# Two graph-attention layers on one core: neighbour sums begun during the projection, for 17 targets in place of 13

## The chip, the core and the metric

The kernel runs as one program on one core of a Trainium2 chip. The core has a matrix engine (PE; PEld is its loading of weights), a vector engine (DVE), a scalar engine (ACT), GpSimd (POOL), a sync engine (SP) that here only issues transfers, and sixteen DMA engines shared by all queues. The metric is the device time of one execution in microseconds, as the median of the runs shown.

## What is computed

Two graph attention layers over N = 3327 nodes with 1024 features, each followed by a residual sum and a normalization. Layer 0 has 8 heads of 128, layer 1 has one head. The graph is sparse: a node has some 16 neighbours. Cut to what matters:

```python
h = (x @ W).reshape(C, H, D)                       # layer 0
e = leaky_relu(alpha_src[:, :, None] + alpha_dst[:, None, :], 0.2)
attn = softmax(where(adj == 0, -inf, e))           # per head
x = layernorm(x + concat_heads(attn @ h))
h = x @ W1                                         # layer 1
attn = softmax(where(adj > 0, leaky_relu(f1 + f2.T, 0.2), -9e15))
x = layernorm(x + relu(attn @ h))
```

## The kernel before

Nodes are handled in NT = 26 tiles of 128. The program has two arms and picks one by a flag that it computes (L923, L929); with these inputs the sparse arm runs. Its work falls into three stages.

**Projection (L514 to L926).** For each tile t, x is loaded three tiles ahead (`load_x`), transposed on PE (`flip`), and multiplied with W in three cuts (`project`, L546); `keep` takes the cuts out of PSUM with ACT (L560 to L565) and SP writes the tile's rows to the table `h0_d` in HBM (L568). The last 16 columns of a row hold the exponentials of the scores. Each cut calls `pace()` after every second multiply, so a tile has 12 slots. `pace` advances two generators that fill the time beside the multiplies:

- `listing` (L582) makes lists of edges, one target tile per round. The mask tile `ad` (3327 int32 columns of `adj`, turned to bytes by the POOL queue's transfer, `load_mask`, L535; three buffers) loses its own diagonal on POOL (`clear`, L339), is counted on ACT (`words`, L350, L352) and folded three times on DVE (L357) into words of 104. `ends` and `ends2` turn counts into places with one small PE multiply each (L366, L391), an ACT copy (L371, L392) and a row of small POOL operations. `keys` and `columns` take the largest of the keys on DVE (L309, L311); `ways`, `places`, `spread`, `give`, `take` and `sources` bring each edge to its slot (L451 on ACT, L470 on PE) and end with the row numbers `idx` (L511, DVE). In a round, mask t + 4 is cleared and counted. `factors` (L330 to L334, ACT and POOL) puts the target's scores beside the edges; `keep` calls it.
- `sums_so_far` (L629) starts when tile 13 is projected. The first 13 tiles of the table are then written, and edges are ordered so that blocks 0 and 1 of a target's four blocks (and one further block for what is left over) have their sources there. For the first EARLY = 13 targets it gathers these two blocks from `h0_d`, four indirect transfers each by POOL (L641), into a ring of three buffers, `near[1]`, `far`, `near[0]`; DVE makes the weighted marks `e` (L658 to L662), PE multiplies (L671, 32 multiplies a block, in the trace two records each; L719 and L737 for the denominators), and the half sum goes to `half_d` (L727). It fetches two blocks ahead and has 12 steps per target, one per slot.

What is left of both generators runs off behind the last projection (L924).

**Layer 0 (L1057 to L1200).** Targets run through a pipeline in an order written at L1381 to L1385. A late target (13 to 25) gathers blocks 0 to 3 with four indirect transfers each and the end block with one (L1034), 17 in all; an early one gathers blocks 2, 3 and the end, 9 in all, and reads its half sum (L1076). Each also reads x, its own row of h and a list, and writes `y_d`. Five buffers `src` hold gathered blocks. The order is late, early, late, early, for eleven pairs, then early 11 and 12, then late 24 and 25. L1168 on DVE is the start of a target's end.

**Layer 1 (L1202 to L1301)** gathers from `y_d` in the same way, sums (L1258) and multiplies with W1 (L1290). It waits for all of layer 0.

The engines work their instructions in program order. The order of the projection stage is what the calls of `pace` make of it at build time.

Of the kernel before, what the change touches and what calls it, by code (L numbers as in the profile page):

```python
# [9 lines left out]
F32 = mybir.dt.float32  # L10
# [9 lines left out]
P = 128  # L20
# [6 lines left out]
def kernel(  # L27
# [57 lines left out]
    EARLY = NTH  # L85
# [35 lines left out]
    cnt = const.tile([P, NT, 4], F32, name="cnt")  # L121
# [193 lines left out]
    class Edges:  # L315
# [6 lines left out]
        def __init__(self, ph, t):  # L322
            self.ph, self.t = ph, t
            self.d, self.deg, self.end2 = cnt[:, t, :2], cnt[:, t, 2:3], cnt[:, t, 3:]
# [18 lines left out]
        def words(self, ad, junk):  # L343
# [7 lines left out]
            self.deg_b = sbuf("deg_b", [P, 2], 4, dt=BF16)  # L351
            nc.scalar.activation(self.deg_b, self.d, AF.Copy)  # L352
            w = ad.bitcast(I32)
            for n in range(3):
                m = WD >> n
                half = sbuf(f"wd{n}", [P, m], 4 if n == 2 else 1, dt=I32)
# [6 lines left out]
        def ends(self, tri_b):  # L363
# [4 lines left out]
            end, off, low, high = (v[:, n : n + 2] for n in (0, 2, 4, 6))  # L368
            self.mid, self.over, self.offs = v[:, 8:10], v[:, 10:12], v[:, 12:14]
            self.more, self.mid2, self.start, self.off2 = (v[:, n : n + 1] for n in range(14, 18))  # L370
# [5 lines left out]
            nc.gpsimd.tensor_scalar(high, end, float(HG2), None, op0=OP.max)  # L376
            nc.gpsimd.tensor_tensor(self.over, high, low, OP.subtract)
            nc.gpsimd.tensor_tensor(self.more, self.over[:, :1], self.over[:, 1:], OP.add)
            nc.gpsimd.tensor_copy(self.more_b, self.more)
            nc.gpsimd.tensor_tensor(self.deg, self.d[:, :1], self.d[:, 1:], OP.add)  # L380
            nc.gpsimd.tensor_copy(self.offs, off)
            nc.gpsimd.tensor_tensor(self.offs[:, :1], off[:, :1], self.d[:, 1:], OP.subtract)
            nc.gpsimd.tensor_tensor(self.offs[:, :1], self.offs[:, :1], self.over[:, :1], OP.subtract)
            mv = self.ph.mvs[self.t % 4][:, :, : XB + 1 : XB]
            nc.gpsimd.tensor_copy(mv[:, 0, :], self.offs)
            nc.gpsimd.tensor_tensor(mv[:, 1, :], self.offs, mv[:, 0, :], OP.subtract)

        def ends2(self, all_b):
# [6 lines left out]
            nc.gpsimd.tensor_tensor(self.off2, self.start, self.d[:, 1:], OP.subtract)  # L395
            nc.gpsimd.tensor_tensor(self.off2, self.off2, self.over[:, 1:], OP.add)
# [117 lines left out]
    with ExitStack() as own, tc.manual_schedule():  # L514
        ph = Phase(own, "proj", {"A": 2, "T": 1})
        pool, bank = ph.pool, ph.bank
        part = Phase(own, "part", {})
        opening = ExitStack()
# [35 lines left out]
        def keep(t, c):  # L554
            if t not in hts:
                hts[t] = ph.sbuf("ht", [P, HW0], 3)
            ht, acc, c0 = hts[t], accs.pop((t, c)), CUTS0[c]
            m = min(CUTS0[c + 1], D) - c0
            if c == 2:
                nc.scalar.activation(sd0[:, t].rearrange("p a h -> p (a h)"), acc[:, m:], AF.Copy)  # L560
                lists[t].factors()
# [13 lines left out]
        def count(t):  # L575
            if t < NT:
                clear(t)
                lists[t].words(ads.pop(t), junk)
                if t:
                    load_mask(t + 2)  # L580
# [962 lines left out]
```

## Time and profile before

| what | value |
|---|---|
| median of 6 runs | 1913.58 us (1908.11 to 1918.13) |
| profiled execution | 1917.7 us, span 1916.0 us |
| granted TensorE clock, mean | 0.916 |
| busy share of the span | PE 86%, PEld 49%, DVE 62%, ACT 27%, POOL 57% |
| moved by DMA | 586.89 MB, 306 GB/s |
| share of 16 DMA engines | POOL queue (q0) 68.7%, SP queue (q1) 18.1% |

A page is one profiled execution; times are microseconds from the start of its span. A share of busy time is a mean over the stages. "Idle before" in a row of a group is time in which that engine did nothing just before an instruction of the group, with what ended most of it. In a table of waits, `PE dd L366 <- ACT deg_b L352: 11.6, 8, 3.1` reads: before its instruction at line 366, PE waited for what ACT makes at line 352, for 11.6 us in all, 8 times, at most 3.1 us. In the timeline a row has its start, how long it took, engine, line, operation, output and input.

### The profile page before, as it was taken

To read this page: it belongs to the slowest core of one execution; us is meant where nothing else is said; L and a number is where in the kernel's file an instruction comes from. 1 tells how busy PE (TensorE), PEld (TensorE's weight loads), DVE (VectorE), ACT (ScalarE), POOL (GpSimd) and SP (SyncE) were. 2 spreads that over 40 slices of the span, in tenths; PEclk is the share of its full clock that TensorE was granted. 3 is DMA by queue.
4 is the path that set the end of the run, shared out by engine and by line. 5 is a ranking of instruction groups with operands and counts; after the bars stand their busy time and mean duration, and the time that the engine had idled before them with its cause. 6 is when DMAs were issued, how large, how long until landed. Compare 5 with 4: busy or idle time off the path is not lost.

```text
span 1916.0 us, 35590 instructions
## 1 busy us (share of the span) xinstructions
PE 1645.4 (86%) x13168; PEld 933.1 (49%) x13168; DVE 1183.7 (62%) x3261; ACT 515.3 (27%) x1519; POOL 1093.2 (57%) x1580
## 2 busy tenths in 40 slices
PE   8899899999985877777777767589999999999998
PEld 5566565656653544444454444234444444444443
DVE  6799998878746676667777686324443444444443
ACT  5656554545321222222222223001111111111110
POOL 4533356656556656555665556366666666666650
PEclk9999999999996877888778878689999999999999
DMA  6556778987789999999999999689999999999990
GB/s 181 100 124 140 130 213 250 261 261 244 242 295 353 382 364 383 352 365 353 361 385 360 348 343 314 250 323 387 384 386 362 386 394 385 372 374 386 369 357 33
DMA packets 187161, 586.89 MB, mean 306 GB/s; under 512 B 36610, under 2 KB 46620, under 8 KB 186978
## 3 DMA queue, kind: packets, MB, share of 16 engines
q0 software_dynamic: 131056, 457.74, 68.7%
q1 hardware_dynamic: 55922, 126.78, 18.1%
q8 instruction: 107, 1.75, 0.4%
q14 instruction: 76, 0.62, 0.1%
HBM read 587.80 MB, written 51.23 MB: 334 GB/s over the span
## 4 chain that ended last, share of the span: by engine, by line
PE 44%; issue 9%; DVE 9%; DMA 3%; ACT 2%; another core or an unknown queue 1%; POOL 1%; DVEq 0%; SPq 0%; ACTq 0%; POOLq 0%
PE mm L1290 19%; PE acc L1258 13%; PE acc L1146 7%; DVE e L1115 2%; PE acc L1127 2%; PE acc L1135 1%; PE tr L197 1%; DVE y L1178 1%; DMA end<-h_d,idx 1%; ACT own L1093 1%; DVE pr L1185 1%; DVE st L218 1%; DVE own L1089 1%; DMA own<-h_d 1%
## 5 line engine op out<-in xcount | busy, mean ns | idle before, releaser
L546 PE MATMUL mm<-wt,xT 128*128 128x347 f32 (+1 forms) x1248 | 412.0, 472 | 3.6 <-DMA wt<-in_L_gnn_W_dram 3.3
L1290 PE MATMUL mm<-wt,xT 128*128 128x512 f32 x832 | 390.6, 607 | 3.7 <-issue 3.7
L1034 POOL DMA_INDIRECT src<-y_d,idx x248 | 250.5, 1010 | 144.2 <-PE acc L1258 64.3
L546 PEld LDWEIGHTS mm<-wt,xT 128*128 128x128 f32 x1248 | 227.0, 193 | 120.7 <-issue 24.6
L1034 POOL DMA_INDIRECT src<-h_d,idx x184 | 199.0, 1081 | 140.7 <-PE acc L1146 62.9
L1290 PEld LDWEIGHTS mm<-wt,xT 128*128 128x128 f32 x832 | 150.3, 190 | 204.9 <-issue 200.4
L1293 DVE SCALAR_TENSOR_TENSOR o<-mm,y 128x512 f32<-128x512 f32 x52 | 36.0, 692 | 343.7 <-PE mm L1290 150.4
L1034 POOL DMA_INDIRECT near<-y_d,idx x168 | 170.1, 1012 | 89.6 <-PE acc L1258 42.1
L1146 PE MATMUL acc<-src,e 128*32 128x128 f32 x2944 | 161.0, 335 | 40.3 <-issue 39.2
L1034 POOL DMA_INDIRECT near<-h_d,idx x120 | 125.7, 1048 | 92.4 <-PE acc L1146 44.6
L1115 DVE TENSOR_TENSOR e<-oh,way 128x1024 f32<-128x1024 f32 x104 | 127.1, 1222 | 61.2 <-ACT w L1113 37.0
L1146 PEld LDWEIGHTS acc<-src,e 128*32 128x32 f32 x2944 | 112.0, 135 | 102.8 <-issue 88.2
L1258 PE MATMUL acc<-src,es 128*32 128x341 f32 x1488 | 135.8, 471 | 21.8 <-DVE es L1249 20.7
L1146 PE MATMUL acc<-near,e 128*32 128x128 f32 x2048 | 115.2, 341 | 43.3 <-issue 31.3
L200 ACT ACTIVATE xT<-tr 128x512 f32<-128x512 f32 x104 | 62.3, 600 | 269.7 <-PE tr L197 196.6
L1272 ACT ACTIVATE z<-y,ri 128x342 f32<-128x342 f32 (+1 forms) x78 | 39.5, 569 | 323.5 <-DVE ri L1268 190.6
L1146 PEld LDWEIGHTS acc<-near,e 128*32 128x32 f32 x2048 | 80.5, 137 | 87.9 <-issue 77.9
L1113 ACT ACTIVATE w<-way 128x32 f32<-128x32 f32 x104 | 20.2, 194 | 324.3 <-DVE way L1111 195.8
L641 POOL DMA_INDIRECT near<-h_d,idx x76 | 83.0, 1092 | 29.1 <-issue 19.9
L1258 PEld LDWEIGHTS acc<-src,es 128*32 128x32 f32 x1488 | 49.5, 112 | 97.4 <-issue 54.0
L1258 PE MATMUL acc<-near,es 128*32 128x342 f32 (+1 forms) x1008 | 88.8, 460 | 4.2 <-DVE way L1246 2.4
L350 ACT ACTIVATE junk<-ad 128x1664 uint8<-128x1664 uint8 x52 | 82.5, 1587 | 4.7 <-POOL ad L339 3.5
(241 smaller groups left out, 2548.6 us busy)
## 6 DMA issues: line engine op xcount, KB each, us to landing
h_d<-ht SPq DMA_DIRECT2D x26, 520.0 KB
own<-h_d SPq DMA_DIRECT2D x26, 520.0 KB
y_d<-y SPq DMA_DIRECT2D x26, 514.0 KB
y<-y_d SPq DMA_DIRECT2D x26, 514.0 KB
x<-in_x_dram SPq DMA_DIRECT2D x25, 512.0 KB
y<-in_x_dram SPq DMA_DIRECT2D x25, 512.0 KB
out_dram<-o SPq DMA_DIRECT2D x25, 512.0 KB
ad<-in_adj_dram POOLq DMA_DIRECT2D x25, 415.9 KB
```

The costliest lines, as they stand in the source:

```text
L200: nc.scalar.activation(part, tr, AF.Copy)
L350: nc.scalar.activation(junk, ad[:, n * THR : (n + 1) * THR], AF.Copy, accum_out=self.d[:, n : n + 1])
L546: nc.tensor.matmul(acc, xT[t][:, k, :], wt[:, k, CUTS0[c] : CUTS0[c + 1]], start=k == 0, stop=k == KT - 1)
L641: nc.gpsimd.indirect_dma_start(out=src[n % 3][:, g, :], out_offset=None, in_=h0_d[:THR, :], in_offset=bass.IndirectOffsetOnAxis(ap=idx[:, ...
L1034: nc.gpsimd.indirect_dma_start(out=s[:, g, :w], out_offset=None, in_=table[:n, :], in_offset=bass.IndirectOffsetOnAxis(ap=idx[:, t, b * NG ...
L1115: nc.vector.tensor_tensor(e, oh.unsqueeze(2).to_broadcast([P, ng, H, wide]), wp.unsqueeze(3).to_broadcast([P, ng, H, wide]), OP.mult,)
L1127: nc.tensor.matmul(self.acc[j - 1].rearrange("p h d -> p (h d)"), ident, self.h[:, (j - 1) * HALF : j * HALF], start=False, stop=False,)
L1146: nc.tensor.matmul(self.acc[h // 4][g * GT : (g + 1) * GT, h % 4, :], e[:, g, h, :], rowsof[:, g, h, :], start=first and h % 4 == 0, stop= ...
L1258: nc.tensor.matmul(self.acc[c][to, :m], es[:, g, :], s[:, g, CUTS[c] : CUTS[c + 1]], start=b == 0, stop=b == EB,)
L1272: nc.scalar.activation(z[:, cut], self.res[:, cut], AF.Copy, scale=ri[:, 1:2])
L1290: nc.tensor.matmul(acc, xT[:, k, :], wt1[:, k, half], start=k == 0, stop=k == KT - 1)
L1293: nc.vector.scalar_tensor_tensor(o[:, half], acc, 0.0, res[:, half], op0=OP.max, op1=OP.add)
```

## The change

- EARLY becomes 17. Four more targets get their blocks 0 and 1 summed during the projection, and `half_d` and `dens` grow with it. The order of layer 0 becomes: each of the first seven late targets (17 to 23), followed by two or three early ones, then late 24 and 25.
- Masks leave the rounds of `listing`. A generator of its own, `counting`, clears one mask or counts one in every third slot, so that all masks are read and folded by about the time the first thirteen tiles are projected. The last fold is kept in a ring of 16, as are the counts `deg_b`; the second fold is made in place. `need` sees that a count is there before `ends` uses it.
- `listing` has 7 steps a round in place of 8 and is paced at two rates: three sevenths of its steps up to the slot at which early sums begin, the rest after it.
- `factors` moves from `keep` into the step with `ways`. The wait for the next tile's scores stands before that step.
- `sums_so_far` has 9 steps per target: the pauses behind each block's fetch and one behind the store of the half sum are taken out. Its ring turns so that the blocks fetched for the first target of layer 0 land in `near[0]` and `near[1]`. `far` is allotted at the start and also holds tile 0 of h, and `ht` has two buffers in place of three.
- In `ends` three of fourteen POOL operations go, in `ends2` one; the sum of the two counts is made once for all targets at the end, by one DVE operation.

The diff, cut:

```diff
-    EARLY = NTH
+    EARLY = NTH + 4
...
-            self.deg_b = sbuf("deg_b", [P, 2], 4, dt=BF16)
+            self.deg_b = sbuf("deg_b", [P, 2], 16, dt=BF16)
...
-                half = sbuf(f"wd{n}", [P, m], 4 if n == 2 else 1, dt=I32)
+                half = w[:, :m] if n == 1 else sbuf(f"wd{n}", [P, m], 16 if n == 2 else 1, dt=I32)
...
-                hts[t] = ph.sbuf("ht", [P, HW0], 3)
+                hts[t] = ph.sbuf("ht", [P, HW0], 2) if t else far[:, 0, :]
...
-                lists[t].factors()
...
         def count(t):
-            if t < NT:
+            counted.add(t)
+            clear(t)
+            lists[t].words(ads.pop(t), junk)
+            if t:
+                load_mask(t + 2)
+
+        def counting():
+
+            for t in range(3, NT):
                 clear(t)
-                lists[t].words(ads.pop(t), junk)
-                if t:
-                    load_mask(t + 2)
+                yield
+                count(t)
+                yield
+
+        def need(t):
+            while t not in counted:
+                next(counts)
...
                     if s == 1 and 2 < t + 3 < NT:
+                        need(t + 3)
                         lists[t + 3].ends(tri_b)
-                    if s == 2 and t >= 0:
-                        clear(t + 4)
                     if s == 3 and 2 < t + 3 < NT:
                         lists[t + 3].ends2(all_b)
+                    yield
+                while new and t + 1 not in scored:
                     yield
...
                 if new:
                     new.ways()
+                    new.factors()
                 yield
                 if old:
                     old.sources()
-                    yield
-                while new and t + 1 not in scored:
                     yield
                 if new:
                     new.places()
                     new.spread()
                     yield
-                count(t + 4)
-                yield
...
+        total, turn_at = 7 * NT + 5, ((NT // 2 - 3) * 12 + 12, (NT - 3) * 12 + 8)
         def pace():
             slots[0] += 1
-            while done[0] * slots[1] < slots[0] * (8 * (NT + 1)):
+            n = slots[0]
+            if n % 3 == 0:
+                next(counts, None)
+            first = 3 * total // 7
+            if n <= turn_at[0]:
+                aim = 4 + (first - 4) * n / turn_at[0]
+            else:
+                aim = first + (total - first) * (n - turn_at[0]) / (turn_at[1] - turn_at[0])
+            while done[0] < aim:
...
-            src = [near[1], part.pool.tile([P, NG, HG], F32, bufs=1, name="far"), near[0]]
+            src = [near[0], near[1], far]
+            k = EARLY * HB % 3
+            src = src[-k:] + src[:-k] if k else src
...
                     if n:
                         fetch(n + 2)
-                    yield
                     if b == 0 and owed:
...
                 res.pop(0)
-                yield
                 if s + 1 < EARLY:
                     oh = marks(s + 1)
...
-        for k in range(NTH - 2):
-            order += [late[k], early[k]]
-        order += early[NTH - 2 :] + late[NTH - 2 :]
+        n = len(late) - 2
+        for k in range(n):
+            order += [late[k], *early[k * EARLY // n : (k + 1) * EARLY // n]]
+        order += late[n:]
```

## The prediction

> **What bounds the kernel now.** I read the busy table by stage first, because the page's shares mix stages with different limits; the cuts are where the trace shows a handover (72 us: third tile scored; 259 us: thirteenth scored; 575 us: last early sum; 1207 us: last target of layer 0). Columns: stage, length, busy us of PE, PEld, DVE, ACT, POOL, granted clock, DMA share, GB/s.
>
> ```profile
> 72.23:259.00 186.77, 173.11 (x781) 114.59 (x782) 167.20 (x482) 109.67 (x355) 70.44 (x323) 0.97 0.63 123
> 259.00:575.00 316.00, 289.95 (x2670) 189.63 (x2668) 238.56 (x654) 139.03 (x438) 190.10 (x395) 0.99 0.85 263
> 575.00:1207.00 632.00, 453.29 (x5823) 303.02 (x5823) 436.57 (x1127) 142.12 (x413) 369.95 (x347) 0.80 0.95 359
> ```
>
> Three limits show. In layer 0 (575 to 1207) DMA is 0.95 busy and no engine over 0.72: transfers set the pace. In projection's second part PE is 0.92 busy: PE sets it. In its first part PE is 0.93 and DVE 0.90 busy, so I asked what PE waited for between 100 and 259 us:
>
> ```profile
> PE dd L366 <- ACT deg_b L352: 11.6, 8, 3.1
> ```
>
> That is nearly all of PE's idle time there: `ends` waits for a count that ACT does late. Behind it stands DVE: in the timeline, listing's last instruction (L511) comes every 15.75 us from 102 to 261 us, and one listing's DVE work is about that long.
>
> Tile spacings come from the scores (L560; the first row below is tile 5, then 13, 14 and 25):
>
> ```profile
> 117.84 0.24 ACT L560 ACTIVATE sd<-mm 128x16 f32<-128x16 f32 x1
> ...
> 259.03 0.24 ACT L560 ACTIVATE sd<-mm 128x16 f32<-128x16 f32 x1
> 277.92 0.16 ACT L560 ACTIVATE sd<-mm 128x16 f32<-128x16 f32 x1
> ...
> 542.73 0.18 ACT L560 ACTIVATE sd<-mm 128x16 f32<-128x16 f32 x1 [1.75 <-PE mm L546]
> ```
>
> Without early sums a tile takes (259.03 - 117.84)/8 = 17.65 us; with them (542.73 - 277.92)/11 = 24.07 us.
>
> For layer 0 I read each target's finish (L1168) in the timeline. The rows end targets 22, 9, 23, 10, 11, 12, 24, 25; those under 13 are early:
>
> ```profile
> 1046.94 0.27 DVE L1168 TENSOR_TENSOR met<-den,meets 32x128 f32<-32x128 f32 x1
> 1065.86 0.27 DVE L1168 TENSOR_TENSOR met<-den,meets 32x128 f32<-32x128 f32 x1
> 1094.34 0.27 DVE L1168 TENSOR_TENSOR met<-den,meets 32x128 f32<-32x128 f32 x1
> 1115.72 0.27 DVE L1168 TENSOR_TENSOR met<-den,meets 32x128 f32<-32x128 f32 x1
> 1135.47 0.27 DVE L1168 TENSOR_TENSOR met<-den,meets 32x128 f32<-32x128 f32 x1
> 1154.29 0.27 DVE L1168 TENSOR_TENSOR met<-den,meets 32x128 f32<-32x128 f32 x1
> 1178.94 0.27 DVE L1168 TENSOR_TENSOR met<-den,meets 32x128 f32<-32x128 f32 x1
> ```
>
> An early target costs 18.9 to 21.4 us here, a late one 24.7 to 28.5. Over all 25 spacings (628.45 to 1206.87) 13 early ones take 257.3 us (19.8 each), 12 late ones 321.1 (26.8 each).
>
> **Layer 0: four late targets become early.** Each loses two blocks, 8 indirect DMAs, and gains one 512 KB read of its half sum. The DMA view of 628 to 1207 us gives the prices (packets, MB, share of the 16 engines):
>
> ```profile
> q0 software_dynamic: 46237, 160.83, 73.7%
> q1 hardware_dynamic: 15614, 45.96, 20.7%
> ```
>
> q0: 0.737 x 578 us / 160.83 MB = 2.65 us per MB; 317 gathers moved it, so 1.34 us each. q1: 2.60 us per MB, so 1.37 us for a half sum. By DMA alone a target saves 8 x 1.34 - 1.37 = 9.4 us, four 37.6. But an early target's DMA is only 9 x 1.34 + 4 x 1.37 + 0.2 = 17.7 us against 19.8 measured, so early targets don't get all of it. I sum by the new order instead: seven late targets are each followed by two or three early ones (four times two, three times three), then two late ones. The trace has one group of three early and a late (1094.34 to 1178.94): 84.6 us. For two early and a late I take the mean pair, 46.6, and one early after an early, (19.8 + 18.8)/2 = 19.3: 65.9. So 4 x 65.9 + 3 x 84.6 + 27.9 (the last) = 545.3 against 578.4: **-33 us**. Bounds: -39 if DMA alone decides (37.6/0.95), -6 if each of the ten extra earlies costs the longest spacing seen, 21.8. I take -33, since all early-after-early rows we have are under 20.
>
> **Projection's second part: eight more blocks.** The instruction order of the two kernels puts 256 more multiplies (two records each) between the first sum and the last projection, and the same 96 behind it, so the drain stays. From matmul start to matmul start a record takes 46 ns there (56.3 us for 1236), so a target's 128 cost 5.9 us, and its L719 and L737 0.8: 6.7. By tiles it is 24.07 - 17.0 = 7.1 us (17.0 is 17.65 less half of PE's wait on the count, 11.6 us over 9 tiles). Four targets: 27 to 28; I take **+28**. All of it is on the path, PE being the limit.
>
> What moves with it: masks leave this part. DVE loses nine folds (0.58 + 0.38 + 0.27 = 1.2 us each), ACT nine counts (3.6 us each), the queue nine loads; DVE gains 4 x 3.9 us of weights and marks and 0.9 of a listing (13 us). Net DVE +17 us on a stage that grows by 28, so it stays near 0.75. DMA: 32 gathers x 1.5 us (0.675 x 316 us shared by 112 gathers and nine loads of 4.8 us) = +48, four half sums' writes and lists +7, less 43 for the masks: +12, share still near 0.85. PE's wait on counts here (2.8 us) goes, and I give one more microsecond of small waits: **-3**.
>
> Two yields fewer per target between weights and sums make DVE's cover for L662 two slots (about 4.3 us) instead of three (6 us). In the trace the spread is bare: of the 26 blocks, e is ready 2 to 8 us before PE takes it in most, but 0.0 to 0.7 us before in five (blocks 0, 1, 5, 12, 24). If those lose a slot of 2 us, 34 x 5/26 = 6.5 blocks cost 13; if DVE is nearer now that folds are gone, nothing. I take **+4**. The gather's cover falls from 11 slots to 8, 22 to 17 us; its last issue is 7 to 23 us before use and its rows land 2.4 to 10.4 us after that issue, the longest while a mask load shares the queue. With masks gone I price it at nothing; without that cover it would be up to 3 us a block.
>
> On POOL every gather is an instruction too: 32 x 1.3 us = 42 us on an engine 0.60 busy here, with `factors` (four operations) now behind them and ACT's L451 behind `factors`. The removed operations of `ends` and `ends2` give back 104 x 0.27 = 28 us. I price this at nothing, because POOL waits (L331, L373) for more than 50 us of the stage; if the cover is gone, ACT's evacuation (L565) is late next, and PE with it.
>
> **Projection's first part: all masks.** Nine more loads, 43 us of DMA on a share of 0.63: 0.86. They have nine slots (13 us) between issue and `clear`; the trace's loads take 6.5 to 9.4 us here, once 12.9. Counting ahead takes the 11.6 us wait off PE. What is late next is DVE: a listing takes 12.1 slots instead of 10.5, its DVE time 15.75 - 1.2 + 2 x 1.2 = 17.0 us, so 16.9 us a tile, and PE's own work is about 17.0. I take 17.1 against 17.65 over ten tiles: **-5**. Bounds -12 (the whole wait) and +6 (ACT, 0.59 busy, gets 0.9 more counts a tile, 3.1 us, is then near 0.79 busy and holds L565 back).
>
> Sum: -33 + 28 - 3 + 4 - 5 = **-9 us**. The profiled execution took 1917.7 us (span 1916.0 and 1.7 around it), 4.1 above the median of six, 1913.58. So 1908.7 on its account, 1904.6 on the median's.
>
> **One rule against the change.** The gathers in projection are 1092 ns (near) and 1033 ns (far) with DVE 0.75 busy, those of layer 0 1075 and 1044 with DVE 0.69:
>
> ```profile
> L641 POOL DMA_INDIRECT near<-h_d,idx x76 | 83.0, 1092 | 29.1 <-issue 19.9 <-PE part L671 6.6 <-PE tr L197 0.8
> L1034 POOL DMA_INDIRECT src<-h_d,idx x166 | 178.4, 1075 | 123.9 <-PE acc L1146 61.1 <-issue 28.7 <-PE den L1156 19.9
> ```
>
> The Trainium skill, "SBUF — State Buffer" (the box on DVE blocking DMA), says that a transfer issued by GpSimd starves while DVE holds the port that they share, and gives 3100 ns in place of 620. Were that so here, moving 32 gathers beside a busy DVE would cost 32 x 2.5 = 80 us of POOL's queue, an estimate from that page, and the change would lose. The rows show no such difference, and the sum goes by them.
>
> **Rivals.**
> (a) DMA decides layer 0 in full, and counting ahead frees the first part: -39 + 29 - 10 = -20, 1893. For it: share 0.95. Against: 17.7 against 19.8.
> (b) Runs of early targets are bound by their own chain (DVE is 0.81 busy between 1100 and 1150 us, and L1083 waits 45.7 us in all for ACT's L1082). At 20.3 us each instead of 19.3, ten extra ones give back 10 us, layer 0 saves 23, and the change comes out at +1: no change, 1914.6. Against: the two rows that there are, 19.8 and 18.8.
> (c) Slower: PE waits in the second part for DVE's e, now two slots ahead. The mechanism is L662 behind a listing step of 2 to 3 us; the price is 34 blocks by the mean stall. At 0.12 us it is my +4; at 0.38 us the sum is zero; from 0.55 us on it is over 0.3% slower; at 0.8 us it is +14, 1928. For it: five bare blocks of 26. Against: PE waited 0.5 us for L662 in all of 259 to 575 us. Tiles would then be 27.2 us or more apart.
>
> **Chances.** Forecast (1897 to 1908) 0.46, (a) 0.16, (b) 0.22, (c) 0.16. A difference of 0.3% (5.7 us) is about what a measurement of this kernel can tell from no change. Faster takes the forecast and (a): 0.62; same 0.22; slower 0.16. The range reaches into (a) and (b) and to the near end of (c): 1888 to 1923.
>
> **What would show it.** Right: tiles 14 to 25 some 26.4 us apart, tiles 5 to 13 some 17.1 with no wait on L352; layer 0 some 545 us from its first finish to its last, DMA share still over 0.9. Wrong: early-after-early finishes over 20.5 us, `PE part L671 <- DVE e L662` over 15 us, or ACT waiting for POOL at L451.

## The result and the profile after

The changed kernel takes 1921.38 us (median of 34 runs, 1911.99 to 1931.67) against 1913.68 us (median of 76 runs of the kernel before, 1901.16 to 1924.62): a ratio of 1.0043, 95% interval 1.0031 to 1.0054. **It is slower, by 0.43% in that ratio and 7.7 us between the medians, where 9 us faster was forecast.** Beside the kernel before on two further occasions the ratio was 1.0066 and 1.0054, so the sign is not chance.

The profiled execution took 1921.7 us (span 1920.0), 4.0 us more than that of before. By the stages that the prediction cut, in us:

| stage | before | after | difference | forecast |
|---|---|---|---|---|
| start to tile 13 scored | 259.0 | 252.0 | -7.0 | -5 |
| tile 13 to the first finish of layer 0 | 369.4 | 403.2 | +33.8 | +29 |
| first to last finish of layer 0 | 578.4 | 558.2 | -20.2 | -33 |
| last finish to the end | 709.1 | 706.6 | -2.5 | 0 |
| sum | 1916.0 | 1920.0 | +4.0 | -9 |

Profiled executions lie some 4 us about their medians (here 4.0 above it for before, 0.4 for after), so a difference of 3 us in one stage is read with care, and one of 13 is not scatter.

The table by windows, cut at the same handovers. Columns: stage, length, busy us of PE, PEld, DVE, ACT, POOL, granted clock, DMA share, GB/s. The second row has its counterpart in before's third (359 GB/s, share 0.95 there).

```profile
252.01:600.00 347.99, 319.73 (x3219) 209.01 (x3217) 258.65 (x705) 113.41 (x430) 225.74 (x387) 0.96 0.82 282
655.20:1213.40 558.20, 402.91 (x4982) 272.41 (x4974) 400.11 (x1059) 125.33 (x352) 304.07 (x289) 0.79 0.93 343
```

The second part still has PE at 0.92 and DVE at 0.74, as forecast. In layer 0 8% fewer bytes move (343 x 558 = 191.5 MB in place of 359 x 578 = 207.6), in 3.5% less time.

Scores of tiles (after): tile 4, 13, 14 and 25.

```profile
106.41 0.17 ACT L561 ACTIVATE sd<-mm 128x16 f32<-128x16 f32 x1
...
252.01 0.17 ACT L561 ACTIVATE sd<-mm 128x16 f32<-128x16 f32 x1
270.10 0.18 ACT L561 ACTIVATE sd<-mm 128x16 f32<-128x16 f32 x1
...
566.09 0.19 ACT L561 ACTIVATE sd<-mm 128x16 f32<-128x16 f32 x1 [2.35 <-PE mm L547]
```

Tiles 14 to 25 come (566.09 - 270.10)/11 = 26.9 us apart (24.07 before, 26.4 forecast); tiles 4 to 13 come 16.2 apart.

In layer 0 the prediction read finishes. L1188 is now that row; these end targets 12, 13, 23, 14, 15, 16, of which 23 is late:

```profile
1059.40 0.27 DVE L1188 TENSOR_TENSOR met<-den,meets 32x128 f32<-32x128 f32 x1
1078.72 0.27 DVE L1188 TENSOR_TENSOR met<-den,meets 32x128 f32<-32x128 f32 x1
1105.54 0.27 DVE L1188 TENSOR_TENSOR met<-den,meets 32x128 f32<-32x128 f32 x1
1126.40 0.27 DVE L1188 TENSOR_TENSOR met<-den,meets 32x128 f32<-32x128 f32 x1
1146.15 0.27 DVE L1188 TENSOR_TENSOR met<-den,meets 32x128 f32<-32x128 f32 x1
1164.98 0.27 DVE L1188 TENSOR_TENSOR met<-den,meets 32x128 f32<-32x128 f32 x1
```

By these rows the targets take 19.3 (13), 26.8, 20.9, 19.8 and 18.8 us. But DVE takes a target's own row before the *previous* target's finish, and for an early target that step holds the 2.2 us in which the half sum is added (L1109). So by finishes an early target's half sum is charged to the target ahead of it: the late one before a run looks dearer, the last early one of a run cheaper. L1105 (L1085 before) stands just ahead of the half sum and is a cleaner mark; the same stretch by it, for targets 13, 23, 14, 15, 16 and 24:

```profile
1054.84 0.23 DVE L1105 TENSOR_SCALAR es<-es,loop 128x8 f32<-128x8 f32 x1
1074.75 0.23 DVE L1105 TENSOR_SCALAR es<-es,loop 128x8 f32<-128x8 f32 x1
1100.98 0.23 DVE L1105 TENSOR_SCALAR es<-es,loop 128x8 f32<-128x8 f32 x1
1121.67 0.35 DVE L1105 TENSOR_SCALAR es<-es,loop 128x8 f32<-128x8 f32 x1
1141.59 0.23 DVE L1105 TENSOR_SCALAR es<-es,loop 128x8 f32<-128x8 f32 x1
1161.01 0.23 DVE L1105 TENSOR_SCALAR es<-es,loop 128x8 f32<-128x8 f32 x1
```

Now the early targets behind early ones (13, 15, 16) take 19.9, 19.9 and 19.4, the late one (23) 26.2 and the early one behind it (14) 20.7. Means by this mark over all of layer 0, in us (number of them):

| from own row to own row | before | after |
|---|---|---|
| late, behind an early one | 26.1 (11) | 26.7 (7) |
| early, behind a late one | 20.6 (11) | 22.4 (7) |
| early, behind an early one | 19.6 (2) | 19.7 (10) |

An early target behind another is 19.4 to 19.9 us with hardly any spread, in before and in after alike. A stretch held by a transfer queue that all targets share would be expected to vary with its neighbours; so the experiments start from here.

### The profile page after: what moved, and what is told of

Its sections match the earlier page's. It is cut to its first block, busy times and chain, and to the rows that moved or that the text cites. A ratio compares the mean times of both kernels' runs of the same rounds, so it can differ in the third digit from the quotient of the medians.

```text
span 1920.0 us, 35535 instructions
## 1 busy us (share of the span) xinstructions
PE 1649.7 (86%) x13172; PEld 938.9 (49%) x13172; DVE 1198.8 (62%) x3306; ACT 504.4 (26%) x1491; POOL 1093.5 (57%) x1476
## 3 DMA queue, kind: packets, MB, share of 16 engines
q1 hardware_dynamic: 57650, 131.10, 18.7%
## 4 chain that ended last, share of the span: by engine, by line
PE 62%; DVE 18%; issue 10%; ACT 5%; DMA 3%; another core or an unknown queue 1%; POOL 1%; DVEq 0%; SPq 0%; ACTq 0%; POOLq 0%
PE mm L1310 19%; PE acc L1278 13%; PE mm L547 12%; PE acc L1166 6%; PE part L692 4%; PE tr L197 2%; DVE e L1135 2%; ACT junk L350 2%; DVE y L1198 2%; PE acc L1147 1%; DVE pr L1205 1%; DVE st L218 1%; DVE own L1109 1%; PE acc L1155 1%
## 5 line engine op out<-in xcount | busy, mean ns | idle before, releaser
L547 PE MATMUL mm<-wt,xT 128*128 128x347 f32 (+1 forms) x1248 | 417.0, 475 | 3.6 <-DMA wt<-in_L_gnn_W_dram 2.9
L547 PEld LDWEIGHTS mm<-wt,xT 128*128 128x128 f32 x1248 | 228.1, 194 | 119.7 <-issue 23.7
L1054 POOL DMA_INDIRECT src<-h_d,idx x168 | 176.9, 1053 | 144.6 <-PE acc L1166 71.0
L1166 PE MATMUL acc<-src,e 128*32 128x128 f32 x2688 | 156.4, 360 | 30.7 <-issue 29.3
L1054 POOL DMA_INDIRECT near<-h_d,idx x104 | 110.1, 1059 | 86.7 <-PE acc L1166 47.2
L1135 DVE TENSOR_TENSOR e<-oh,way 128x1024 f32<-128x1024 f32 x96 | 117.3, 1222 | 50.1 <-ACT w L1133 29.7
L1278 PE MATMUL acc<-src,es 128*32 128x341 f32 x1488 | 132.1, 464 | 16.1 <-DVE es L1269 12.5
L1166 PE MATMUL acc<-near,e 128*32 128x128 f32 x1792 | 105.9, 352 | 37.0 <-issue 25.8
L662 POOL DMA_INDIRECT near<-h_d,idx x96 | 106.6, 1111 | 38.8 <-issue 26.4
L1166 PEld LDWEIGHTS acc<-near,e 128*32 128x32 f32 x1792 | 73.9, 142 | 77.3 <-issue 69.9
L1133 ACT ACTIVATE w<-way 128x32 f32<-128x32 f32 x96 | 18.8, 196 | 337.3 <-DVE way L1131 254.8
```

The lines of the kernel that those rows point to most:

```text
L547: nc.tensor.matmul(acc, xT[t][:, k, :], wt[:, k, CUTS0[c] : CUTS0[c + 1]], start=k == 0, stop=k == KT - 1)
L662: nc.gpsimd.indirect_dma_start(out=src[n % 3][:, g, :], out_offset=None, in_=h0_d[:THR, :], in_offset=bass.IndirectOffsetOnAxis(ap=idx[:, ...
L1054: nc.gpsimd.indirect_dma_start(out=s[:, g, :w], out_offset=None, in_=table[:n, :], in_offset=bass.IndirectOffsetOnAxis(ap=idx[:, t, b * NG ...
L1135: nc.vector.tensor_tensor(e, oh.unsqueeze(2).to_broadcast([P, ng, H, wide]), wp.unsqueeze(3).to_broadcast([P, ng, H, wide]), OP.mult,)
L1166: nc.tensor.matmul(self.acc[h // 4][g * GT : (g + 1) * GT, h % 4, :], e[:, g, h, :], rowsof[:, g, h, :], start=first and h % 4 == 0, stop= ...
L1278: nc.tensor.matmul(self.acc[c][to, :m], es[:, g, :], s[:, g, CUTS[c] : CUTS[c + 1]], start=b == 0, stop=b == EB,)
```

## The experiments

**My theory:** runs of early targets are not held by transfers but by a chain of their own on DVE, so with 17 of them the gain in layer 0 stops at about 20 us, while each half sum costs the second part over 9. **The transfer rival:** transfers hold layer 0 (share 0.93), and the missing 13 us are lost in the order of the targets. **The masks rival:** the missing time lies in the masks' half of the change. Where the expectations below name theories by letters, the letters are theirs. Ratios are against the kernel before on the same chip; the kernel before itself differs by chip.

| run | edit, in words | its median | before there | ratio (95%) |
|---|---|---|---|---|
| masks_13 | after, 13 early, before's order | 1929.49 | 1936.79 | 0.9958 (0.9924-0.9993) |
| sums_17 | before, 17 early | 1941.61 | 1936.79 | 1.0022 (0.9999-1.0046) |
| pairs_17 | after, pairs first | 1927.96 | 1936.79 | 0.9958 (0.9925-0.9992) |
| load_early | after, all prepared a block earlier | 1919.91 | 1936.79 | 0.9912 (0.9881-0.9943) |
| after_2 | none | 1814.10 | 1802.33 | 1.0066 (1.0053-1.0079) |
| load_l0 | the same, layer 0 alone | 1791.56 | 1802.33 | 0.9934 (0.9920-0.9947) |
| own_pool | half sum added by POOL | 1843.03 | 1802.33 | 1.0227 (1.0213-1.0240) |
| load_l0_b | before, with load_l0's edit | 1798.98 | 1802.33 | 0.9980 (0.9969-0.9989) |
| before_2 | before, none | 1803.26 | 1803.13 | 0.9999 (0.9985-1.0012) |
| after_3 | none | 1812.39 | 1803.13 | 1.0054 (1.0034-1.0073) |
| light_17 | after, half the gathered bytes | 1815.88 | 1803.13 | 1.0073 (1.0056-1.0091) |
| best_17 | load_l0 and pairs_17 | 1801.36 | 1803.13 | 0.9992 (0.9980-1.0005) |
| marks_l0 | after, only the marks earlier | 1894.91 | 1913.64 | 0.9897 (0.9868-0.9927) |
| loads_l0 | after, only the transfers earlier | 1926.27 | 1913.64 | 1.0062 (1.0039-1.0085) |
| masks_13_b | masks_13 again | 1912.01 | 1913.64 | 0.9995 (0.9974-1.0017) |
| masks_13_load | masks_13 and load_l0 | 1887.69 | 1913.64 | 0.9862 (0.9838-0.9886) |
| half_pe_17 | load_l0, half sum added by PE | 1916.30 | 1936.61 | 0.9896 (0.9863-0.9930) |
| half_pe_13 | the same with 13 early | 1902.02 | 1936.61 | 0.9830 (0.9796-0.9863) |

### The two halves of the change

masks_13 and masks_13_b are the same edit of after, on two chips. sums_17 is the kernel before with 17 early targets, and the order, ring and fewer pauses of after; its masks stay in the rounds.

```diff
-    EARLY = NTH + 4
+    EARLY = NTH
...
-            order += [late[k], *early[k * EARLY // n : (k + 1) * EARLY // n]]
-        order += late[n:]
+            order += [late[k], early[k]]
+        order += early[n:] + late[n:]
```

> The changed kernel with EARLY back at 13 and layer 0 in the order of the kernel before; masks, pacing and the nine steps per target stay as changed. Theory 1 (the loss is in the trade: four more early sums cost the projection some 28 us and give back only some 20 in layer 0): the projection keeps what the early masks gain, 7 us by tile 13, its tiles 14 to 25 come back to some 23.5 to 24 us apart, layer 0 takes 578 us from first to last finish again, and the time is 1902 to 1909, faster than the kernel before by 5 to 12 us. Theory 2 (reading and folding all masks early is what costs, by DMA and ACT): 1914 or more, with tile 13 no earlier than 259 us or tiles 14 to 25 over 24.5 us apart.

> The changed kernel with EARLY back at 13 and layer 0 in the order of the kernel before, once more (its first trace was of a disturbed execution). The early masks alone: tile 13 scored 4 to 7 us earlier than before, the projection's second part and layer 0 as before, time 0.2 to 0.4% under the kernel before. If it is 0.2% or less, the early masks are worth next to nothing, and the whole loss of the change is the trade less that.

> The kernel before with EARLY at 17, and of the change only what that needs: the order of layer 0, the turned ring, nine steps per target. Masks stay in the rounds of the listing. Theory 1: the projection's second part gets the four sums (27 to 30 us) with the masks still in it, layer 0 saves some 20; 1920 to 1932. Theory 2: without the early masks the sums pay, 1895 to 1912.

The masks alone gave 0.9958 on one chip and 0.9995 on the other: a small gain or none. The stages are read from masks_13_b: tile 13 at 255.3 us (259.0 in before), the second part 365.6 (369.4), layer 0 576.9 (578.4). Against masks_13_b, after has +37.6 us in the second part and -18.7 in layer 0. The masks rival falls: moving the masks costs nothing on the whole, and **four more half sums cost 9.4 us each there and give back 4.7 each**. (loads_l0 below, with 17 early targets on the chip of masks_13_b, has 404.6 and 554.8, which gives the same picture.) With the other stages (-3.3 and -1.7) the profiled executions are 13.9 us apart; the medians differ by 9.4 us, masks_13_b's profile having been 4.1 us under its median. The sign is the same. sums_17, the other half alone, has the same shape: second part 402.0, layer 0 564.3.

### The order

```diff
-            order += [late[k], *early[k * EARLY // n : (k + 1) * EARLY // n]]
-        order += late[n:]
+            order += [late[k], early[k]]
+        order += early[n:] + late[n:]
```

> The changed kernel with layer 0 in pairs: late and early in turn for seven pairs, then the other ten early targets in a row, then two late ones. If an early target costs some 21 us only where another early one follows (its successor's own transfers are then issued late), ten in a row cost 10 x 21 and pairs cost 46.6: layer 0 takes 560 to 570 us, the time is 1921 to 1932. If an early one after an early one takes 19.3 whatever surrounds it, layer 0 takes some 548 us, the time is some 1911. If only the DMA queue's bytes count, the order makes no difference: 558 us, 1921.

Layer 0 is 552.3 us, between the expectation's 548 and 560, against 564.3 in sums_17 on the same chip, and the kernel comes out 0.4% ahead of before. Early targets behind early ones are still 19.7. Both orders have seven late-early pairs, ten early behind early; half of the difference lies at the start, where the grouped order's first early target takes 28.4 us and the pairs' 22.5. So the order is worth some of the missing time on this chip. On a faster chip and beside load_l0's edit, in best_17 below, it is worth nothing.

### What holds an early target: bytes?

light_17 gathers only the first half of each row in layer 0, so the second half of the rows and the weights in them are not right; all instructions stay.

```diff
-            self.src[b] = gather(h0_d, HW0, self.t, b)
+            self.src[b] = gather(h0_d, HW0 // 2, self.t, b)
```

> The changed kernel once more, unedited, as the measure for the others on this chip. Expected: 0.2 to 0.6% slower than the kernel before.

> The kernel before, unedited, for a trace from the same chip as the others of this call. By the timeline from one target's own-row step to the next, early targets should take 19.6 to 20.6 us whatever the chip, late ones what DMA allows: 26 to 27 us on a chip where the kernel takes some 1914 us, 22 to 23 where it takes some 1802.

> The changed kernel, unedited, on the same chip. Theory (the trade depends on how slow DMA is): early targets 19.7 us again; layer 0 saves, against before_2, four times the gap between late and early less some 1 us for each of the seven early targets that follow a late one. With late targets at 26 us that is 15 to 22 us and the kernel is 0.2 to 0.5% slower than before; with late ones at 22 us it is 3 to 9 us and 0.5 to 0.8% slower; with late ones at 29 us it is 25 us or more and the kernel is no slower.

> The changed kernel with layer 0's gathers moving only the first half of each row (520 of 1040 numbers; the other half of the buffers holds what stood there, so the second half of the heads and the weights of these blocks are not computed from the right rows). Some 75 MB less DMA in layer 0. If early targets are held by their own chain (own row on DVE, weights, sums), they stay at 19 to 20 us and late ones fall to 21 to 22, the floor seen on the chip with fast DMA; layer 0 takes some 495 to 510 us. If their bytes hold them, early targets fall to 15 to 17 us and layer 0 to under 460.

Layer 0 by windows, light_17 and then the unedited after_3 on the same chip:

```profile
660.00:1140.00 480.00, 338.96 (x4753) 254.27 (x4745) 378.89 (x1004) 120.30 (x341) 287.50 (x269) 0.76 0.73 242
```

```profile
660.00:1140.00 480.00, 323.24 (x4678) 241.46 (x4678) 377.21 (x1005) 119.28 (x338) 285.51 (x267) 0.79 0.97 375
```

The DMA share falls from 0.97 to 0.73 and the time does not move: layer 0 502.7 against 505.9, the whole 1.0073 against 1.0054. DVE's busy time (378.9 and 377.2) is what the two rows share. Own-row marks of light_17: three spacings, of the early target behind a late one and of two early ones behind it:

```profile
896.27 0.23 DVE L1107 TENSOR_SCALAR es<-es,loop 128x8 f32<-128x8 f32 x1
915.97 0.36 DVE L1107 TENSOR_SCALAR es<-es,loop 128x8 f32<-128x8 f32 x1
935.74 0.23 DVE L1107 TENSOR_SCALAR es<-es,loop 128x8 f32<-128x8 f32 x1
955.39 0.23 DVE L1107 TENSOR_SCALAR es<-es,loop 128x8 f32<-128x8 f32 x1
```

19.7, 19.8, 19.7: what they are with all bytes. The transfer rival falls for early targets, and on this chip for late ones too (22.1 against 22.4). A DMA share of 0.97 was a busy unit beside the bound, not the bound. The chips differ in late targets: 26 to 27 us on the chip of the first profile, 22.4 here. So the premise that a late target costs 7 us more than an early one belongs to the first chip. Here the difference is 3.0 us (before_2, 22.7 and 19.7), and the change costs more: layer 0 gains 13.6 us (519.5 to 505.9) and the second part loses 28.9.

That slower transfers make late targets dearer on the first chip was not tried, and the rows there point to PE. Target 23, a late one, from own row to own row, in after and then in after_3 (columns as above):

```profile
1074.75:1100.98 26.23, 21.31 (x313) 14.57 (x309) 16.44 (x41) 6.86 (x21) 14.41 (x14) 0.79 0.90 336
```

```profile
1008.35:1030.02 21.67, 18.39 (x302) 14.01 (x298) 16.45 (x42) 6.85 (x21) 13.80 (x13) 0.74 0.87 330
```

The same multiplies (some records are missing) keep PE busy 21.3 us on the first chip and 18.4 here, at no lower clock. On the first chip PE also stands idle between them with "issue" as the reason, which is time in which it waited for nothing that the profile shows: 3.3 us in target 23, and in all of after's layer 0

```profile
PE acc L1166 <- issue: 49.3, 128, 1.1
```

after_3 has no such row. Before, after and all runs of the table on chips where the kernel before takes 1914 us or more have 49 to 72 us in this row in layer 0, all those on the chips with 1802 us at most 0.7. At the end of target 23 DVE waits for ACT's exponential (L1102), which stands on ACT behind a copy (L1219) that waits for PE:

```profile
1100.17 0.27 ACT L1219 ACTIVATE line<-tr 1x128 f32<-1x128 f32 x1 [4.97 <-PE tr L1217]
1100.57 0.17 DVE L1103 TENSOR_TENSOR es<-es,own 128x8 f32<-128x8 f32 x1 [5.79 <-ACT es L1102]
```

So a late target on the first chip looks held by PE, which is 0.94 busy or at "issue" there. No edit here was aimed at that, and what makes PE slower on those chips stays open.

### What holds an early target: DVE's chain

The timeline of DVE for one early target of after (target 13; the larger operations and the waits):

```profile
1054.43 0.17 DVE L1103 TENSOR_TENSOR es<-es,own 128x8 f32<-128x8 f32 x1 [1.23 <-ACT es L1102]
...
1055.10 2.19 DVE L1109 SCALAR_TENSOR_TENSOR own<-own,es,half 128x128 f32<-128x128 f32 x8
...
1058.26 1.22 DVE L1135 TENSOR_TENSOR e<-oh,way 128x1024 f32<-128x1024 f32 x1 [0.32 <-ACT w L1133]
...
1060.79 2.16 DVE L1198 SCALAR_TENSOR_TENSOR y<-acc,ri,y 128x128 f32<-128x128 f32 x8
...
1062.87 0.68 DVE L1070 TENSOR_TENSOR oh<-io_t,tgt 128x512 f32<-128x512 f32 x1
...
1068.68 1.23 DVE L1205 SCALAR_TENSOR_TENSOR pr<-y,wa 128x1024 f32<-128x1024 f32 x1
...
1074.35 0.17 DVE L1103 TENSOR_TENSOR es<-es,own 128x8 f32<-128x8 f32 x1 [1.39 <-ACT es L1102]
```

DVE is busy 16.0 us of the 19.7, and in a late target 16.5 to 16.7: two blocks less save 3.2 us, own row and half sum cost 2.4 more. **Making a late target early takes next to nothing off DVE.** The wait in the last row recurs in each target: DVE needs an exponential of ACT for the own row and has nothing to do meanwhile. load_early prepares the next target (its transfers and, on DVE, its marks `oh`) at the first block of the target before and not half way, in both layers; in layer 1 this overwrites residual rows that are still needed, so they are wrong there. load_l0 does it in layer 0 alone, load_l0_b does it to the kernel before.

```diff
-                    if j == nb // 2 and after:
+                    if j == (0 if isinstance(after, Layer0) else nb // 2) and after:
                         after.prepare()
```

> The changed kernel with each target's own transfers (x, own row, half sum) and marks issued at the first block of the target before it, not at its middle block; both tables of layer 0 and layer 1 are served so. If early targets are held by these transfers (DVE waits 53 us in layer 0 for the first operation on the own row), layer 0 loses 10 to 25 us and the time is 1896 to 1911. If that wait only stands beside another limit, the time stays within 5 us of 1921.

> The changed kernel with each target's own transfers and marks issued at the first block of the target before it, in layer 0 alone. Theory A (early targets are held by their own transfers, which are issued only two blocks ahead): layer 0 takes 530 to 545 us from first to last finish, DVE's wait before the first operation on the own row falls from 53 us to under 15, and the kernel is 0.6 to 1.2% faster than the changed kernel. Theory B (they are held by DVE's 2.2 us on the own row): layer 0 stays at 555 us or more.

> The kernel before with the same early issue of own transfers in layer 0. It says whether the hold is there for 13 early targets as well. Theory A: layer 0 takes 555 to 568 us in place of 578, less of a gain than with 17 early targets (13 of 17), 0.5 to 1% faster than before; the trade of four more early sums then gives back some 25 us in layer 0, not 20. Theory B: no difference, 578 us.

Early targets fall to 19.0 us, late ones to 21.0 (load_l0; 19.8 and 22.5 in after_2 beside it), and the whole from 1.0066 to 0.9934. In the kernel before the same edit gives 0.2%, less than expected: its early targets fall to 18.9 as well, but its late ones stay at 22.8 (22.7 in before_2). Why they stay no run shows. Two things had been moved, transfers and marks, so the next pair parts them:

```diff
+                    if j == 0 and isinstance(after, Layer0):
+                        after.mark()
                     if j == nb // 2 and after:
                         after.prepare()
```

(marks_l0; `prepare` no longer makes the marks in layer 0, but for the first target. In loads_l0 `prepare` comes at block 0 and `mark` at nb // 2.)

> The changed kernel with only the marks (two DVE operations, 0.97 us) of each layer 0 target made at the first block of the target before it, ahead of that target's own-row step; its transfers stay at the middle block. Theory M (DVE stands idle 1.4 us per target until ACT's L1102 is done, and the marks fill that gap): the own-row wait falls to 0.5 us, early targets take 18.9 us instead of 19.7 and the kernel gains 0.8 to 1.2% on the changed kernel. Theory T (the transfers came too late): early targets stay at 19.7.

> The changed kernel with only the transfers of each layer 0 target issued at the first block of the target before it; the marks stay at the middle block. Theory T: early targets take 18.9 us and the kernel gains 0.8 to 1.2% on the changed kernel. Theory M: early targets stay at 19.7 where DMA is fast; only where DMA is slow does some of the wait for the own row go, up to 0.5%.

The wait of DVE for ACT at the own row, 600 to 1215 us, in after, marks_l0 and loads_l0 (total us, times, longest):

```profile
DVE es L1103 <- ACT es L1102: 53.5, 21, 7.2
```

```profile
DVE es L1107 <- ACT es L1106: 14.8, 18, 6.7
```

```profile
DVE es L1107 <- ACT es L1106: 50.0, 22, 6.6
```

Marks alone give it all (0.9897; layer 0 524.4 us; early 18.8, late 24.2), transfers alone nothing (1.0062; on the same chip layer 0 554.8, early 19.7, late 25.5). Two DVE operations that do not depend on ACT fill the gap. The stage flatters the edit, as the first finish comes 6 us later with it (second part 410.2 against 404.6); by medians the whole is 31.4 us under loads_l0. Own-row marks of marks_l0; the first spacing is a late target, the second the early one behind it, the next two early behind early:

```profile
908.40 0.23 DVE L1109 TENSOR_SCALAR es<-es,loop 128x8 f32<-128x8 f32 x1
931.78 0.23 DVE L1109 TENSOR_SCALAR es<-es,loop 128x8 f32<-128x8 f32 x1
953.89 0.35 DVE L1109 TENSOR_SCALAR es<-es,loop 128x8 f32<-128x8 f32 x1
972.62 0.23 DVE L1109 TENSOR_SCALAR es<-es,loop 128x8 f32<-128x8 f32 x1
991.60 0.23 DVE L1109 TENSOR_SCALAR es<-es,loop 128x8 f32<-128x8 f32 x1
```

My theory holds this far: reordering DVE's own work, with every byte and transfer where it was, moves the early targets that halving the bytes could not move.

### Taking the half sum off DVE

own_pool lets ACT scale the own row of every target and POOL add the half sum.

```diff
+                    nc.scalar.activation(h[:, d], h[:, d], AF.Copy, scale=es[:, n : n + 1])
+                if t < EARLY:
+                    nc.gpsimd.tensor_tensor(h[:, :D], h[:, :D], self.half, OP.add)
```

> The changed kernel with the own row of early targets scaled by ACT (eight instructions, as for late targets) and the half sum added by POOL (one addition of 1024), so that DVE is rid of eight instructions, 2.2 us, per early target. Theory B: 17 targets lose 1 to 2 us each, layer 0 takes 525 to 542 us, 0.8 to 1.6% faster than the changed kernel. Theory A: no gain, layer 0 at 553 us or more; and it is slower if the addition holds gathers back on POOL.

Early targets behind early ones got slower, 22.2 us, and the trace shows a wait that the edit made:

```profile
DVE es L1111 <- ACT own L1108: 43.2, 17, 2.6
```

The sum of the denominators overwrites `es` while ACT still reads it. The run says nothing on the DVE work taken away. half_pe_17 mends that: load_l0's edit, the sum in a tile of its own, and the half sum added by PE with an identity, two multiplies more.

```diff
+                    self.es = sbuf("es2", [P, H], 2)
...
+                    if self.t < EARLY:
+                        nc.tensor.matmul(
+                            self.acc[j - 1].rearrange("p h d -> p (h d)"), ident,
+                            self.half[:, (j - 1) * HALF : j * HALF], start=False, stop=False,
+                        )
```

> The changed kernel with transfers and marks a block earlier in layer 0, and the own row of early targets taken off DVE: ACT scales it, as for late targets, and PE adds the half sum into the same sums with the identity, as it adds the own row (two multiplies more per early target); the denominator's sum goes to a tile of its own, so that nothing on DVE waits for ACT. Theory D (early targets are held by DVE's own work, 18.9 us of it without a gap): they take 16.5 to 17.5 us, late ones stay, layer 0 is 20 to 35 us shorter than with the early marks alone, time 0.970 to 0.982 of the kernel before. If PE or transfers hold them next, they stay at 18.5 us or more and the time at 0.985 to 0.993.

DVE's busy time per early target falls from 16.1 to 13.9 us, but the period only from 18.9 to 18.2, so theory D's 16.5 to 17.5 is missed. (Its 18.9 us "without a gap" was not so either: in load_l0 DVE is busy 16.1 us of an early target and waits some 2.4.) Something else holds at 18.0. The DMA share is 0.96 over 660 to 1140 us, and 9 gathers and the reads at the prediction's prices make 17.7, which fits but was not tried. ACT is a second candidate, since it scales these own rows now: DVE's waits for ACT's weights come to 48.0 us (620 to 1150 us), where load_early has 30.6 (655 to 1200). What holds then stays open.

### Does 17 beat 13 in any version?

> The changed kernel with own transfers issued a block earlier in layer 0 (as in load_l0) and layer 0 in pairs (as in pairs_17). Early issue gave 1.3% against the changed kernel, pairs some 0.6% beside the other order where DMA was slow. If both gains come from the same waits, this is no faster than early issue alone: 0.993 of before. If they add, 0.988 to 0.991.

> The same with own transfers and marks a block earlier in layer 0. Against the kernel before: 0.2% from early issue (as measured with 13 sums) and what masks_13_b shows; 0.994 to 0.997. With 17 sums the same edit gave 0.9934; if this is no slower than that, the four additional sums pay nothing even with the shortened targets.

> The same with EARLY 13 and pairs. Theory D: 13 early targets gain 1.5 to 2.4 us each where transfers allow it; 0.974 to 0.984 of the kernel before. It says once more whether 17 early targets beat 13 when the early target itself is cheap: by theory D the gap between late and early grows by 2 us, 8 us for four targets, which is still less than the 28 to 38 us that their sums cost minus some 20 given back, so 13 stays ahead or level.

best_17 (load_l0 with pairs_17's order) is 0.9992, behind the 0.9934 of load_l0 alone on a like chip: a miss, the two gains don't add, and layer 0 is 491.7 us against 484.1. masks_13_load (masks_13 with load_l0's edit) is 0.9862, ahead of its expectation (the edit is worth 24.3 us there, beside masks_13_b), where marks_l0, the best run with 17 on that chip, is 0.9897. half_pe_13 is 0.9830 and half_pe_17 0.9896 on one chip. Layer 0 is shorter with 17 each time (524.4 against 551.0, 532.5 against 554.7) and the second part longer by more. half_pe_13 has the lowest ratio found, 1.7% under the kernel before, and it has 13 early targets. All this is from the slower chips. On the fast one load_l0, with 17, is ahead of load_l0_b, with 13 and the old masks (1791.56 against 1798.98 us); 13 early targets with the new masks and that edit were not run there, so for fast chips the question is open.

## Why the prediction was wrong, by its steps

- **Layer 0, -33 us: the step that failed.** It came to -20.2 (-18.7 against masks_13_b). The forecast was a sum of finish spacings, and by finishes again the ten early targets behind early ones took 192.8 us where it had 191.2: right. The last target took 20.7 where it had 27.9. What failed is "for two early and a late I take the mean pair, 46.6": a late target and the early one behind it took 49.2, seven of them 344.7 us in place of 326.2. Together +18.5 + 1.6 - 7.2 = +12.9, the whole of 558.2 less 545.3. Of the 18.5, 15 or so lie with the early target behind the late one (22.0 us by finishes, taken as 19.8), and 6 of these with the first alone (25.8).
  Behind it stands "transfers set the pace", read from a share of 0.95 and "no engine over 0.72". That is a mean over two kinds of target. An early one is held by a chain on DVE and ACT, 19.7 us whatever the bytes. A late one and its follower change with the chip: by own rows the pair is 49.1 us in after and 42.2 in after_3, with PE full in the late one of the first. In the followers DVE waits some 2.9 us each for PE's sums (L1192), 0.6 in after_3. That PE holds them is read from the rows, not tried by an edit.
- **The second part, +28 - 3 + 4 = +29.** It came to +33.8. The sums were cheaper than forecast: L692's 512 further records added 19.8 us (76.4 to 96.2, start to start) where 23.6 was forecast. What was not forecast is that the projection's own records (L547) went from 318 to 338 ns, start to start, +10.6 us. Part of that is time in which PE waits behind such a record (3.2 and 8.0 us; 4.0 of it is the wait for `e` of the next point). Records with no wait behind them went from 313 to 323 ns. The granted clock from tile 13 to tile 25 is 0.97 in place of 0.99, which by itself would make 313 some 319 (an estimate). masks_13_b has 320 already, so the masks' half of the change holds most of it. Why the clock was lower no run shows.
- **Two slots of cover for `e`, +4.** Right, also in size. PE's waits between 252 and 600 us in after:

```profile
PE part L692 <- issue: 12.8, 34, 1.0
PE part L692 <- DVE met L727: 4.3, 2, 3.2
PE part L692 <- DVE e L683: 4.0, 2, 2.4
```

  Rival (c) would have needed 19 us or more of the last row. The issue row, 34 blocks at 0.4 us, goes with the number of blocks and was inside the forecast's 6.7 us a target.
- **The gathers at nothing.** Right. Moved beside a busy DVE they take what they take in layer 0: near 1111 ns and far 1079 in the second part, 1053 and 1058 in layer 0.

```profile
L662 POOL DMA_INDIRECT near<-h_d,idx x96 | 106.6, 1111 | 38.8 <-issue 26.4 <-PE part L692 8.9 <-PE mm L547 1.1
L1054 POOL DMA_INDIRECT src<-h_d,idx x152 | 160.0, 1053 | 131.2 <-PE acc L1166 70.7 <-issue 33.8 <-PE den L1176 18.9
```

  The starvation that the Trainium skill, "SBUF — State Buffer" (the box on DVE blocking DMA), warns of is again not to be seen, with DVE 0.74 busy. DVE is nearly as busy in layer 0 (0.72), so the rows only say that nothing of the size of that page's 3100 ns occurs here.
- **The first part, -5.** Right in sum (-7.0), by other terms. The wait on the counts is gone: PE waits 1.4 us for ACT's L451 between 100 and 252 us, and less for all else. Tiles 4 to 13 took 145.6 us in place of 163.5, -17.9: 16.2 a tile, not the 17.1 that I had for DVE's limit. But tile 4 came at 106.4 in place of 95.6. The new pace lets listing start with a burst (three steps at its first slot), and PE waits for it. PE's longest waits from 50 to 120 us, in after and then in before:

```profile
PE xp L470 <- DVE top L309: 4.9, 1, 4.9
PE dd L366 <- ACT deg_b L352: 3.5, 1, 3.5
```

```profile
PE tr L197 <- ACT xT L200: 4.9, 1, 4.9
```

  All its waits there are 11.2 us against 7.5, so they are a part of the 10.8 only; the rest stays open. The score of tile 4 is also read late: PE's 200th multiply of the projection starts 6.6 us later than before (99.0 against 92.4). None of this was in the prediction, and a pace without the burst was not tried.
- **The rivals.** (a) fell with the measured -20.2 and with light_17. (b) named the right mechanism for early targets, their own chain on DVE, and came closest with +1, but by luck: by finishes they took 19.3 us as forecast, not its 20.3, and the loss lies with late targets and their followers and in the second part. The prediction's signs of being wrong would not have told: early-after-early finishes stayed under 20, DVE's `e` cost PE 4.0 us, and ACT's wait for POOL at L451 was 6.8 us in the second part, 6.2 in before.

## What to carry to other kernels

A busy share near 1 names a suspect, not a bound: the spacing that does not vary with position, or the run with half the bytes, tells whether transfers hold. A mean share over steps of two kinds hides the step in which another engine is full: PE was 0.72 busy over before's layer 0, and in late target 23 of after it left 1.6 us of 26.2 unused. Before work is moved from a later stage to an earlier one that is full, count what the move takes off each engine of the later stage; here DVE had 16.5 us per target before the move and 16.0 after. Read a period from a row that begins a step's own work, and when an engine waits about a microsecond for another in each round, first look for independent work of its own to put there: two marks moved one block up gave 1.4% of the kernel (1894.91 us, against 1921.38 on a like chip).

## What was not expected of the hardware

The same kernel differs by chip more than the change moves it: before took 1802, 1803, 1914, 1914, 1937 and 1937 us by median on the occasions shown. Late targets differ with it (26.1 to 26.7 us on the chip of the first profile, 22.4 to 22.7 on a fast one), early ones behind early ones do not (19.6 to 19.8 on all). What sets a chip's pace no run here shows; the plainest mark of it is PE's idle time at "issue", above. In layer 0 the core moved 359 GB/s at a share of 0.95 on the first chip and 393 GB/s at 1.01 on the fast one.

The Trainium skill, "HBM Reference" (Specifications), gives a core about 358 GB/s when its neighbour in the HBM domain streams too, and some 425 alone. The 359 would fit the one; the 393 lies between them. But these are bytes over the length of the stage, nearly the same bytes on both chips (some 208 and 204 MB), and over early target 15 the first chip moves 389 GB/s as well (after):

```profile
1121.67:1141.59 19.92, 13.97 (x165) 10.00 (x161) 16.15 (x45) 4.12 (x11) 10.24 (x10) 0.76 1.01 389
```

So 359 was no limit of that chip. Whether a neighbour was at work no run shows.
